# Three layer norms on VectorE, a pinned start of the stack, and the last pair's GLU one sequence at a time

## The chip, the core and the metric

The kernel runs on one core of a Trainium2 chip. A core has a matrix engine (TensorE, PE in the profile; its weight loads are shown apart as PEld), a vector engine (VectorE, DVE), an activation engine (ScalarE, ACT), a general engine (GpSimd, POOL) and SyncE (SP), which here issues nearly all DMA transfers. Each engine works through its own queue in program order and waits on semaphores for the others. The metric is the device time of one execution in microseconds; lower is better.

## The reference, cut to what matters

Sixteen sequences of 256 tokens with 128 features, float32, go through two blocks.

```python
x = x + causal_attention(layernorm(x))        # 16 heads of 8
x = x + stack(layernorm(x))                   # the stack's own input is the normalised x
# stack: six layers; every step sees shift_tokens(t): the upper 64 features come from the token before
for i in range(6):
    t = local_attention(shift_tokens(t)) + t  # 16 heads of 64, l2-normalised q and k, rotary, windows of 32 with the one before
    t = glu(shift_tokens(t)) + t              # layernorm over features, W1 (128 to 2*341), a*gelu(gate), W2 (341 to 128)
```

The layer norm divides by the root of the variance plus 1e-5. The GLU's gate uses the exact gelu.

## The kernel before, in words

**Two stages.** The first stage does the causal attention. Its loop `for s in range(-3, NSEQ + 3)` runs the steps of several sequences side by side and ends each round with `in_order(traced, True)`, which adds dependencies so that every compute engine takes the instructions of the round in the order in which the program emits them. `normed(s, "b")` (L162 to L179) is the layer norm between the two blocks: statistics and variance plus epsilon on VectorE (L168 to L171), the inverse root as a power on GpSimd (L84, called at L173), and the two halves of `xn_b`, 128x128 each, as a subtract and multiply on GpSimd (L176). `turned(s, "b")` transposes them on TensorE (L190) and ScalarE copies the result into `yT`, the stack's state with features on partitions (L194), one 128x512 tile for two sequences. `finish(s)` (L338 to L347) projects the attention's output, adds it to x and stores that sum to DRAM. `on(s - 3, normed, "b")` for sequence 15 is the last work of this stage.

**The stack.** Steps are numbered n = 16 * layer + sequence, from 0 to N - 1 = 95. `half(n, u)` (L795 to L854) emits half a step, u being 0 or 1, with pieces of several neighbours: `proj_qk` for step n + 2 (L472 to L499), `norms`, `roots`, `spread_k` and `norm_k` for n + 1, `sim`, `soften`, `power` and `proj_v` for n, `share`, `attn_T`, `attn_v` and `project_out` for what is older. Two sequences of one tile form a pair m, and its GLU runs in pieces spread over the following steps: `glu_shift` (L698), `glu_center` (L704), `glu_var` (L714), `glu_norm` (L725), three `glu_part` (L743) and `glu_out` (L760), each 512 columns wide. `leave(s)` (L767) transposes a finished sequence back, adds the sum stored in DRAM and stores the output.

**What sets the order.** For 0 <= n < 96, `in_order` pins each engine to the emitted order. For n = -2 and -1 (the first projections) and for n = 96 to 98 (the last GLU), it does not, and a scheduler places the instructions by its own estimate.

**The start of the stack.** `proj_qk(n, g, k)` multiplies the shifted sequence with one group of weights into PSUM (`qk`, L485), ScalarE squares it (L486), VectorE multiplies it with the rotary tables (`t12`, L487, 128x1024), and GpSimd adds the parts (`sq` at L496, `tq` twice at L499). `t12` has two buffers, so a new one waits until GpSimd has added the one before the last; `tq` has six, so the seventh waits until the first has left by DMA to `us` (L560). PSUM tiles of these steps come from a ring of four (`psum1`). `roots(0)` (L516 to L533) needs ScalarE's copy of the norms (L511), which stands behind the `yT` copies of sequences 14 and 15 on ScalarE; it computes the inverse root on VectorE with a seed and three Newton steps (L521 to L530), and GpSimd spreads it (`kb`, L533). `shift(n)` is two GpSimd copies and a memset (L464 to L466).

**The end of the stack.** ScalarE needs the table of Exp for `power` (L632) and that of Gelu for `glu_part` (L753); a switch is an instruction of its own in its queue. In the last steps, the output projection of sequence 15's second half (`wo`, L688, then the addition at L693) is followed by the GLU of pair 47, which holds sequences 14 and 15.

Of the kernel before, what the change touches and what calls it, by code (L numbers as in the profile page):

```python
# [38 lines left out]
def tile_transformer(  # L39
# [42 lines left out]
    def rsqrt(dst, src):  # L82
        n = dst.shape[-1]
        nc.gpsimd.tensor_tensor(dst, src, mhalf[:, :n], ALU.pow)  # L84

    last = {}
    engines = {e.engine for e in (nc.tensor, nc.vector, nc.scalar, nc.gpsimd)}
# [16 lines left out]
    with ExitStack() as st:  # L104
# [57 lines left out]
        def normed(s, tag):  # L162

            src = x1[s]
            stats = p4.tile([P, 2, 6], F32, tag="stats", name=f"st_{tag}{s}")
            mv = p4.tile([P, 2, 2], F32, tag="mv", name=f"mv_{tag}{s}")
            for t in range(2):
                nc.vector.bn_stats(stats[:, t, :], src[:, t, :])  # L168
                nc.vector.bn_aggr(mv[:, t, :], stats[:, t, :])
            var = p4.tile([P, 2], F32, tag="var", name=f"var_{tag}{s}")  # L170
            nc.vector.tensor_scalar(var, mv[:, :, 1], 1e-5, None, ALU.add)  # L171
            rstd = p4.tile([P, 2], F32, tag="rstd", name=f"rstd_{tag}{s}")
            rsqrt(rstd, var)  # L173
            xn = p2.tile([P, 2, E], F32, tag=f"xn{tag}", name=f"xn_{tag}{s}")
            for t in range(2):
                nc.gpsimd.tensor_scalar(  # L176
                    xn[:, t, :], src[:, t, :], mv[:, t, 0:1], rstd[:, t : t + 1], ALU.subtract, ALU.mult
                )
            xns1[s, tag] = xn  # L179
# [198 lines left out]
    with ExitStack() as st:  # L378
# [18 lines left out]
        def psum1(name):  # L397
            return ps_o.tile([P, 512], F32, tag="o", name=name)
# [115 lines left out]
        def roots(n, n2):  # L514
            ps = psum1(f"nT_{n}").rearrange("p (h g m) -> p h g m", h=4, g=4)
            for h in range(2):  # L516
                nc.tensor.transpose(
                    ps[:, h].rearrange("p g m -> p (g m)"), n2[:, h].rearrange("p a m -> p (a m)"), ident
                )
            x = p2.tile([P, 2, NG, 8], F32, tag="nx", name=f"nx_{n}")  # L520
            nc.vector.tensor_scalar(x, ps[:, 0:2, :, 0:8], 1e-24, None, ALU.max)  # L521

            y = p3.tile([P, 2, NG, 8], F32, tag="rn", name=f"rn_{n}")
            x_, y_ = (v.rearrange("p h g m -> p (h g m)") for v in (x, y))
            nc.vector.tensor_scalar(y_.bitcast(I32), x_.bitcast(I32), -0.5, 1597463007.0, ALU.mult, ALU.add)
            for _ in range(3):
                z = p4.tile([P, 64], F32, tag="nz", name=f"nz_{n}")
                nc.vector.tensor_tensor(z, x_, y_, ALU.mult)
                nc.vector.scalar_tensor_tensor(z, z, -0.5, y_, ALU.mult, ALU.mult)
                nc.vector.scalar_tensor_tensor(y_, z, 1.5, y_, ALU.add, ALU.mult)  # L530
            rn[n] = y
            kb = p1.tile([P, 2, NG, P], F32, tag="kb", name=f"kb_{n}")
            nc.gpsimd.tensor_copy(  # L533
                kb.rearrange("p h g (i d) -> p (h g) i d", d=32),
                y.rearrange("p h g m -> p (h g) m")[:, :, 4:8].unsqueeze(3).to_broadcast([P, 8, 4, 32]),
            )
            kbs[n] = kb
# [157 lines left out]
        x2s, bcs, sms = {}, {}, {}  # L695


        def glu_shift(m):  # L698
            b = m % 8
            x2 = x2s[m] = p1.tile([P, 2 * S], F32, tag="gl", name=f"x2_{m}")  # L700
            for i in range(2):
                shifted(x2[:, i * S : (i + 1) * S], 2 * b + i)

        def glu_center(m):  # L704
            x2 = x2s.pop(m)
            ps = psum1(f"cen_{m}")
            nc.tensor.matmul(ps, center, x2, start=True, stop=True)
            sq2 = p1.tile([P, 2 * S], F32, tag="h1", name=f"fsq_{m}")
            nc.scalar.activation(sq2, ps, AF.Square)
            xc = p1.tile([P, 2 * S], F32, tag="h2", name=f"xc_{m}")  # L710
            nc.scalar.copy(xc, ps)
            xns[m] = sq2, xc

        def glu_var(m):  # L714
            sq2, xc = xns[m]
            pv = psum1(f"pv_{m}")
            for t in range(4):
                nc.tensor.matmul(pv[:, t : t + 1], sq2[:, t * P : (t + 1) * P], mean1, start=True, stop=True)
            var = p4.tile([P, 4], F32, tag="var", name=f"var_{m}")
            nc.vector.tensor_scalar(var, pv[:, :4], 1e-5, None, ALU.add)  # L720
            rstd = p4.tile([P, 4], F32, tag="rstd", name=f"rstd_{m}")
            rsqrt(rstd, var)
            xns[m] = rstd, xc

        def glu_norm(m):  # L725
            l = m // 8
            rstd, xc = xns[m]
            ps = psum1(f"rs_{m}")
            for t in range(4):
# [8 lines left out]
            xn = p1.tile([P, 2 * S], F32, tag="xn", name=f"xn_{m}")  # L738
            nc.vector.tensor_tensor(xn, ps, xc, ALU.mult)
            nc.gpsimd.tensor_scalar(xn, xn, vecs[:, l, V_G : V_G + 1], vecs[:, l, V_B : V_B + 1], ALU.mult, ALU.add)  # L740
            xns[m] = xn

        def glu_part(mm, i):  # L743
            l = mm // 8
            if mm % 8 == 0 and i == 0:
                load_glu(l)
            xn = xns[mm]
            a, m = DI_PARTS[i]
            pg, ph = psum1(f"hg_{mm}_{i}"), psum1(f"ha_{mm}_{i}")
            nc.tensor.matmul(pg[:m], W["1"][:, DI + a : DI + a + m], xn, start=True, stop=True)  # L750
            nc.tensor.matmul(ph[:m], W["1"][:, a : a + m], xn, start=True, stop=True)  # L751
            g = p1.tile([P, 2 * S], F32, tag="gl", name=f"g_{mm}_{i}")
            nc.scalar.activation(g[:m], pg[:m], AF.Gelu, bias=vecs[:m, l, V_B1 + 3 + i : V_B1 + 4 + i])  # L753
            h = p1.tile([P, 2 * S], F32, tag=f"h{i}", name=f"h_{mm}_{i}")
            nc.vector.scalar_tensor_tensor(
                h[:m], ph[:m], vecs[:m, l, V_B1 + i : V_B1 + i + 1], g[:m], ALU.add, ALU.mult
            )
            hs[mm, i] = h

        def glu_out(mm):  # L760
            l, b = divmod(mm, 8)
            ps = psum1(f"w2_{mm}")
            for i, (a, m) in enumerate(DI_PARTS):
                nc.tensor.matmul(ps, W["2"][:m, i, :], hs[mm, i][:m], start=(i == 0), stop=(i == 2))  # L764
            nc.vector.scalar_tensor_tensor(yT[b], ps, vecs[:, l, V_B2 : V_B2 + 1], yT[b], ALU.add, ALU.add)

        def leave(s):  # L767

# [26 lines left out]
        def half(n, u):  # L795
            even = n % 2 == 0
            m = n // 2 - 1 if even else (n - 3) // 2
            glu = lambda m: 0 <= m < N // 2
            i, j = 2 * u, 2 * u + 1
            b, bu = (n, 0) if u else (n - 1, 1)  # L800
            bi, bj = 2 * bu, 2 * bu + 1
# [15 lines left out]
            do(n, soften, i)  # L817
            do(n, soften, j)
            do(n - 1, project_out, u)
            if u:  # L820
                do(n + 3, shift)
                if even and glu(m):
                    glu_shift(m)
            elif has(n + 1):
                roots(n + 1, n2s.pop(n + 1))
            do(b, attn_T, bi)
            do(b, attn_T, bj)
            do(n, proj_v, u, 0)
            do(b, attn_v, bi)
            if not even and u == 0 and glu(m):  # L830
                glu_center(m)
            do(n + 2, proj_qk, j, 0)
# [9 lines left out]
            if u == 0:  # L842
                do(n + 1, spread_k, 0)
                do(n + 1, norm_k, 0)
            do(n, power, i)
            do(n, power, j)
            do(b, attn_v, bj)
            do(*((n, masks, 1) if u == 0 else (n + 1, masks, 0)))
            if even and u and glu(m - 1):
                glu_out(m - 1)  # L850
                if m - 1 >= (DEPTH - 1) * 8:
                    leave(2 * ((m - 1) % 8))
                    leave(2 * ((m - 1) % 8) + 1)
            do(n, proj_v, u, 1)  # L854

        do(0, shift)
        last.clear()
        for n in range(-2, N + 3):
            for u in range(2):
                traced = len(nc.cur_bb.bb.instructions)  # L860
                half(n, u)
                in_order(traced, 0 <= n < N)

# [94 lines left out]
```

## Time and profile before

| | us |
|---|---|
| median of 3 runs | 3634.91 (3633.56 to 3640.62) |
| the profiled execution, as timed | 3631.49 |
| its span, first to last instruction | 3629.4 |
| first stage (causal attention), until its last `x` is added | about 376 |
| last GLU, from its centring to the last addition to `yT` | 3607.28 to 3625.15 |

The mean granted TensorE clock is 0.992. A line of the timeline gives the start in us, the duration in us, the engine with the source line, the operation, output and inputs, shapes and count; in brackets stands how long the engine was idle before and what ended the wait. A float32 matmul shows as two records (passes). `x8` merges eight records of one group.

Each step of the stack takes roughly a 96th of what lies between 440 and 3590 us, with TensorE busy 9 tenths or more in nearly every slice. The two ends are where engines wait for each other: around 368 to 420 us, and from 3587 us on.

### The profile page before, as it was taken

The page shows a single profiled execution, that of the slowest core. Times are in us where ns is not written, and L with a number is a line of the kernel's source. Part 1 is how long each engine was busy: PE and PEld are TensorE (multiplying, and loading weights), DVE is VectorE, ACT ScalarE, POOL GpSimd, SP SyncE. Part 2 cuts the span into 40 slices and gives each one's busy share as a digit, 9 for nine tenths or more (in the row PEclk, how much of TensorE's full clock was granted, in tenths as well). Part 3 has the DMA queues.
Part 4 walks back from the last instruction along what each step waited for, and adds up shares of the span by engine and source line. Part 5 has one row for each costly group of instructions (what it writes and reads, how often), then busy time and mean ns, then how long its engine had stood idle before and what let it go on. Part 6 is the DMA issues. An engine that isn't in the chain of part 4 may idle for free.

```text
span 3629.4 us, 153727 instructions
## 1 busy us (share of the span) xinstructions
PE 3485.9 (96%) x68032; PEld 2451.9 (68%) x68032; DVE 2841.1 (78%) x4866; ACT 1870.2 (52%) x3132; POOL 2592.8 (71%) x2731
## 2 busy tenths in 40 slices
PE   7999799999999999999999999999999999999998
PEld 5777466666666666666666666666676666666665
DVE  5765788887888888888877888877888888888784
ACT  2444355554555555555555555555555555555453
POOL 2221778778777778787777777778777877777772
PEclk9999899999999999999999999999999999999999
DMA  2000333334433334333334433334433343333342
GB/s 82 8 10 10 94 91 100 100 88 110 111 102 84 96 100 111 102 104 100 88 92 117 107 88 99 100 86 116 111 95 83 100 111 93 102 105 102 90 105 60
DMA packets 249444, 331.65 MB, mean 91 GB/s; under 512 B 74446, under 2 KB 105548, under 8 KB 247884
## 3 DMA queue, kind: packets, MB, share of 16 engines
q1 hardware_dynamic: 248060, 321.13, 33.1%
q8 instruction: 536, 8.78, 1.0%
q14 instruction: 128, 1.05, 0.1%
q10 hardware_dynamic: 720, 0.70, 0.1%
HBM read 28.12 MB, written 4.19 MB: 9 GB/s over the span
## 4 chain that ended last, share of the span: by engine, by line
PE 76%; DVE 9%; issue 7%; POOL 3%; ACT 2%; DMA 1%; SPq 0%; POOLq 0%; DVEq 0%; ACTq 0%
PE qk L485 17%; PE po L668 11%; PE v L568 9%; PE wo L688 8%; PE sim L605 6%; PE w L764 4%; PE hg L750 3%; PE ha L751 3%; PE aT L648 3%; PE n L506 2%; DVE tq L558 2%; DVE t L487 2%; PE bc L544 2%; PE sim L585 2%; ACT aT L650 1%
## 5 line engine op out<-in xcount | busy, mean ns | idle before, releaser
L487 DVE TENSOR_TENSOR t<-qk,ab 128x1024 f32<-128x1024 f32 x768 | 915.9, 1218 | 284.1 <-ACT sq L486 252.4
L499 POOL TENSOR_TENSOR tq<-t 128x512 f32<-128x512 f32 x768 | 962.1, 1274 | 85.4 <-DVE t L487 61.0
L485 PE MATMUL qk<-xs,wqk 128*128 128x256 f32 x3072 | 790.9, 393 | 1.6 <-DVE yT L693 1.5
L496 POOL TENSOR_TENSOR sq<-sq 128x512 f32<-128x512 f32 x384 | 489.1, 1274 | 282.3 <-ACT sq L486 272.3
L485 PEld LDWEIGHTS qk<-xs,wqk 128*128 128x128 f32 x3072 | 555.3, 191 | 146.9 <-issue 45.5
L486 ACT ACTIVATE sq<-qk 128x512 f32<-128x512 f32 x768 | 459.4, 599 | 377.3 <-PE qk L485 371.3
L650 ACT COPY aT<-aT 128x512 f32<-128x512 f32 x384 | 207.6, 587 | 599.4 <-PE aT L648 599.2
L668 PEld LDWEIGHTS po<-aT,vs 64*64 64x64 f32 x12288 | 327.8, 135 | 201.2 <-issue 106.8
L568 PE MATMUL v<-wv,xs 128*128 128x512 f32 x768 | 423.8, 634 | 28.1 <-ACT aT L650 21.2
L626 POOL TENSOR_TENSOR sm<-sm,mx 128x512 f32<-128x512 f32 x384 | 396.6, 1045 | 28.1 <-DVE mx L625 27.2
L605 PEld LDWEIGHTS sim<-us 64*32 64x32 f32 x24576 | 260.7, 105 | 205.9 <-issue 189.1
L668 PE MATMUL po<-aT,vs 64*64 64x32 f32 x12288 | 394.6, 222 | 5.2 <-issue 2.6
L668 PE MATMUL po<-aT,vn 64*64 64x32 f32 x12288 | 386.8, 219 | 4.6 <-issue 4.6
L574 ACT COPY vn<-v 128x512 f32<-128x512 f32 x384 | 225.3, 587 | 312.8 <-PE v L568 308.7
L688 PE MATMUL wo<-ao,wout 128*128 128x256 f32 x1536 | 383.2, 392 | 1.0 <-ACT ao L677 1.0
L642 POOL TENSOR_TENSOR ex<-ex,rec 128x512 f32<-128x512 f32 x288 | 317.5, 1116 | 39.7 <-ACT vn L574 18.2
L668 PEld LDWEIGHTS po<-aT,vn 64*64 64x64 f32 x12288 | 330.2, 136 | 5.1 <-issue 4.9
L605 PE MATMUL sim<-us 64*32 64x64 f32 (+1 forms) x24576 | 322.9, 221 | 3.1 <-DMA us<-tq 3.1
L688 PEld LDWEIGHTS wo<-ao,wout 128*128 128x128 f32 x1536 | 276.0, 189 | 49.5 <-ACT ao L677 1.7
L677 ACT COPY ao<-po 128x512 f32<-128x512 f32 x384 | 222.7, 580 | 114.9 <-PE po L668 114.9
L639 DVE TENSOR_REDUCE rec<-ex 128x8 f32<-128x512 f32 x384 | 252.0, 657 | 34.2 <-ACT ex L632 34.2
L625 DVE TENSOR_REDUCE mx<-sm 128x8 f32<-128x512 f32 x384 | 263.5, 686 | 13.3
(122 smaller groups left out, 5244.7 us busy)
## 6 DMA issues: line engine op xcount, KB each, us to landing
us<-tq SPq DMA_DIRECT2D x768, 256.0 KB
vs<-vn SPq DMA_DIRECT2D x384, 192.0 KB
vs<-vn SPq DMA_DIRECT2D x192, 64.0 KB
wqk<-in_f_wqkv_dram SPq DMA_DIRECT2D x96, 64.0 KB
ab<-in_tables_dram SPq DMA_DIRECT2D x6, 1024.0 KB
wv<-in_f_wqkv_dram SPq DMA_DIRECT2D x12, 256.0 KB
wout<-in_f_wo_dram SPq DMA_DIRECT2D x24, 128.0 KB
x<-in_x_dram SPq DMA_DIRECT2D x16, 128.0 KB
```

The lines of the kernel that those rows point to most:

```text
L485: nc.tensor.matmul(ps[:, t * S : t * S + S], W["qk", g][:, k, t, :], xs[n], start=True, stop=True)
L486: nc.scalar.activation(sq2[:, k].rearrange("p t n -> p (t n)"), ps, AF.Square)
L487: nc.vector.tensor_tensor(t12[:, k].rearrange("p f t n -> p f (t n)"), ps.unsqueeze(1).to_broadcast([P, 2, 2 * S]), W["ab", l][:, k].rearr ...
L496: nc.gpsimd.tensor_tensor(sq[n, g], sq2[:, :, 0, :], sq2[:, :, 1, :], ALU.add)
L499: nc.gpsimd.tensor_tensor(tq[n, g][:, t], t12[:, :, 0, t, :], t12[:, :, 1, 1 - t, :], ALU.add)
L568: nc.tensor.matmul(ps, xs[n][:, P * c : P * c + P], W["v"][:, u].rearrange("p g x d -> p (g x d)"), start=True, stop=True)
L605: nc.tensor.matmul(ps[WIN * r : WIN * r + WIN, x, col + first : col + 64], qk[part, g, 0, WIN * c : WIN * c + WIN], qk[part, g, 1, WIN * ( ...
L625: nc.vector.tensor_reduce(mx, seg, AX.X, ALU.max)
L626: nc.gpsimd.tensor_tensor(seg, seg, mx.unsqueeze(2).to_broadcast([P, 8, 64]), ALU.subtract)
L642: on.tensor_tensor(seg, seg, rec.unsqueeze(2).to_broadcast([P, 8, 64]), ALU.mult)
L668: nc.tensor.matmul(po[DH * y : DH * y + DH, h, x, g, WIN * r : WIN * r + WIN], v[64 * h : 64 * h + 64, r // 2, 2 * g + y, x, :], aT[64 * h ...
L688: nc.tensor.matmul(ps[:, :S].rearrange("p (h m) -> p h m", h=2), W["out"][:, g, 2 * u + x, :], a[:, x, :, g, :], start=(j == 0), stop=(j == 3)
```

## The change

Three edits, all at the ends.

**1. Layer norms of sequences 13, 14 and 15** (`normed(s, "b")` for s >= 13). The power on GpSimd becomes a seed and three Newton steps on VectorE, ten instructions on 128x2 (the same helper now also serves `roots`, with one buffer `nz` for its three steps where there were three), and the two 128x128 halves of `xn_b` go to VectorE too.

**2. The first steps of the stack in order.** `in_order(traced, -1 <= n < N)` pins n = -1 as well. The products of step 1, the norms of step 0 and the shift of sequence 2 then stand as emitted.

**3. The end.** `glu` no longer covers pair 47. Its GLU is called as a whole by `glu_all` for one sequence at a time (256 columns): sequence 14 at the end of `half(96, 0)`, sequence 15 in `half(96, 1)` after `project_out(95, 1)`. The last `glu_out` of pair 46 comes one half earlier. The last two `power` (step 95, the second pair of tiles) come before the first two `glu_part` of pair 46 and no longer after them.

```diff
+    def newton(y, x, z):
+        nc.vector.tensor_scalar(y.bitcast(I32), x.bitcast(I32), -0.5, 1597463007.0, ALU.mult, ALU.add)
+        for _ in range(3):
+            nc.vector.tensor_tensor(z, x, y, ALU.mult)
+            nc.vector.scalar_tensor_tensor(z, z, -0.5, y, ALU.mult, ALU.mult)
+            nc.vector.scalar_tensor_tensor(y, z, 1.5, y, ALU.add, ALU.mult)
...
-            rsqrt(rstd, var)
+            last_ones = tag == "b" and s >= NSEQ - 3
+            if last_ones:
+                newton(rstd, var, p4.tile([P, 2], F32, tag="rz", name=f"rz_{s}"))
+            else:
+                rsqrt(rstd, var)
             for t in range(2):
-                nc.gpsimd.tensor_scalar(
+                (nc.vector if last_ones else nc.gpsimd).tensor_scalar(
...
+        def which(m):
+            if isinstance(m, tuple):
+                return m[0] // 8, m[0] % 8, m[1] * S, S, f"{m[0]}_{m[1]}"
+            return m // 8, m % 8, 0, 2 * S, str(m)
...
+        def glu_all(m):
+            glu_shift(m)
+            glu_center(m)
+            glu_var(m)
+            glu_norm(m)
+            for i in range(3):
+                glu_part(m, i)
+            glu_out(m)
+            leave(2 * (m[0] % 8) + m[1])
...
-            glu = lambda m: 0 <= m < N // 2
+            glu = lambda m: 0 <= m < N // 2 - 1
...
             do(n - 1, project_out, u)
+            if n == N and u:
+                glu_all((N // 2 - 1, 1))
...
             do(b, attn_v, bi)
+            if n == N - 1 and u:
+                do(n, power, i)
+                do(n, power, j)
...
-            do(n, power, i)
-            do(n, power, j)
+            if n < N - 1 or u == 0:
+                do(n, power, i)
+                do(n, power, j)
...
-            if even and u and glu(m - 1):
+            if even and u == (n < N) and glu(m - 1):
                 glu_out(m - 1)
...
             do(n, proj_v, u, 1)
+            if n == N and u == 0:
+                glu_all((N // 2 - 1, 0))
...
-                in_order(traced, 0 <= n < N)
+                in_order(traced, -1 <= n < N)
```

The GLU's functions take the width from `which`, so a tuple (47, 0) or (47, 1) runs on 256 columns in tiles of the same size as before.

What the built programs hold, engine by engine, in words. VectorE, at the end of the first stage, has the ten steps for sequence 14 interleaved with the `t12` products of steps 0 and 1: seed, product, first step, product, second step and so on, five of the ten before the last of the products at that place, then the other five, then both halves of `xn_b`, and only then the addition of sequence 15. TensorE has the norms of step 0 before the transposes of sequence 14. GpSimd has the shift of sequence 2 (`xs_2`) between `tq` and `sq` of step 1's third and fourth groups; before, that shift stood in the middle of the first stage. At the end, TensorE's order is:

```
attn_v of step 95, last part
w2 of pair 46 (three matmuls), fin of sequences 12 and 13
cen, pv, rs, hg and ha three times, w2, fin      sequence 14, 256 columns
wo of step 95, second half (four matmuls)
cen, pv, rs, hg and ha three times, w2, fin      sequence 15, 256 columns
```

Everything between, steps 0 to 94, has the same instructions in the same order.

More of the change, by code (lines that the diff above doesn't have):

```diff
@@ L524, in roots @@
             x_, y_ = (v.rearrange("p h g m -> p (h g m)") for v in (x, y))
[L525 to L530, printed above, removed]
+            newton(y_, x_, p4.tile([P, 64], F32, tag="nz", name=f"nz_{n}"))
             rn[n] = y
@@ L695, in tile_transformer @@
         x2s, bcs, sms = {}, {}, {}
+        def which(m):
+            if isinstance(m, tuple):
+                return m[0] // 8, m[0] % 8, m[1] * S, S, f"{m[0]}_{m[1]}"
+            return m // 8, m % 8, 0, 2 * S, str(m)
         def glu_shift(m):
[L699 to L702, printed above, removed]
+            _, b, c0, w, name = which(m)
+            x2 = x2s[m] = p1.tile([P, 2 * S], F32, tag="gl", name=f"x2_{name}")[:, :w]
+            for i in range(w // S):
+                shifted(x2[:, i * S : (i + 1) * S], 2 * b + c0 // S + i)
         def glu_center(m):
             x2 = x2s.pop(m)
-            ps = psum1(f"cen_{m}")
+            _, _, _, w, name = which(m)
+            ps = psum1(f"cen_{name}")[:, :w]
             nc.tensor.matmul(ps, center, x2, start=True, stop=True)
-            sq2 = p1.tile([P, 2 * S], F32, tag="h1", name=f"fsq_{m}")
+            sq2 = p1.tile([P, 2 * S], F32, tag="h1", name=f"fsq_{name}")[:, :w]
             nc.scalar.activation(sq2, ps, AF.Square)
-            xc = p1.tile([P, 2 * S], F32, tag="h2", name=f"xc_{m}")
+            xc = p1.tile([P, 2 * S], F32, tag="h2", name=f"xc_{name}")[:, :w]
             nc.scalar.copy(xc, ps)
@@ L715, in glu_var @@
             sq2, xc = xns[m]
-            pv = psum1(f"pv_{m}")
-            for t in range(4):
+            _, _, _, w, name = which(m)
+            nt = w // P
+            pv = psum1(f"pv_{name}")
+            for t in range(nt):
                 nc.tensor.matmul(pv[:, t : t + 1], sq2[:, t * P : (t + 1) * P], mean1, start=True, stop=True)
-            var = p4.tile([P, 4], F32, tag="var", name=f"var_{m}")
-            nc.vector.tensor_scalar(var, pv[:, :4], 1e-5, None, ALU.add)
-            rstd = p4.tile([P, 4], F32, tag="rstd", name=f"rstd_{m}")
+            var = p4.tile([P, 4], F32, tag="var", name=f"var_{name}")[:, :nt]
+            nc.vector.tensor_scalar(var, pv[:, :nt], 1e-5, None, ALU.add)
+            rstd = p4.tile([P, 4], F32, tag="rstd", name=f"rstd_{name}")[:, :nt]
             rsqrt(rstd, var)
@@ L725, in glu_norm @@
         def glu_norm(m):
-            l = m // 8
+            l, _, _, w, name = which(m)
             rstd, xc = xns[m]
-            ps = psum1(f"rs_{m}")
-            for t in range(4):
+            ps = psum1(f"rs_{name}")[:, :w]
+            for t in range(w // P):
                 nc.tensor.matmul(
@@ L737, in glu_norm @@
                 )
-            xn = p1.tile([P, 2 * S], F32, tag="xn", name=f"xn_{m}")
+            xn = p1.tile([P, 2 * S], F32, tag="xn", name=f"xn_{name}")[:, :w]
             nc.vector.tensor_tensor(xn, ps, xc, ALU.mult)
@@ L743, in glu_part @@
         def glu_part(mm, i):
-            l = mm // 8
-            if mm % 8 == 0 and i == 0:
+            l, b, _, w, name = which(mm)
+            if b == 0 and i == 0:
                 load_glu(l)
@@ L748, in glu_part @@
             a, m = DI_PARTS[i]
-            pg, ph = psum1(f"hg_{mm}_{i}"), psum1(f"ha_{mm}_{i}")
+            pg, ph = psum1(f"hg_{name}_{i}")[:, :w], psum1(f"ha_{name}_{i}")[:, :w]
             nc.tensor.matmul(pg[:m], W["1"][:, DI + a : DI + a + m], xn, start=True, stop=True)
             nc.tensor.matmul(ph[:m], W["1"][:, a : a + m], xn, start=True, stop=True)
-            g = p1.tile([P, 2 * S], F32, tag="gl", name=f"g_{mm}_{i}")
+            g = p1.tile([P, 2 * S], F32, tag="gl", name=f"g_{name}_{i}")[:, :w]
             nc.scalar.activation(g[:m], pg[:m], AF.Gelu, bias=vecs[:m, l, V_B1 + 3 + i : V_B1 + 4 + i])
-            h = p1.tile([P, 2 * S], F32, tag=f"h{i}", name=f"h_{mm}_{i}")
+            h = p1.tile([P, 2 * S], F32, tag=f"h{i}", name=f"h_{name}_{i}")[:, :w]
             nc.vector.scalar_tensor_tensor(
@@ L760, in glu_out @@
         def glu_out(mm):
-            l, b = divmod(mm, 8)
-            ps = psum1(f"w2_{mm}")
+            l, b, c0, w, name = which(mm)
+            ps = psum1(f"w2_{name}")[:, :w]
             for i, (a, m) in enumerate(DI_PARTS):
                 nc.tensor.matmul(ps, W["2"][:m, i, :], hs[mm, i][:m], start=(i == 0), stop=(i == 2))
-            nc.vector.scalar_tensor_tensor(yT[b], ps, vecs[:, l, V_B2 : V_B2 + 1], yT[b], ALU.add, ALU.add)
+            y = yT[b][:, c0 : c0 + w]
+            nc.vector.scalar_tensor_tensor(y, ps, vecs[:, l, V_B2 : V_B2 + 1], y, ALU.add, ALU.add)
+        def glu_all(m):
[7 more added lines that the diff above has]
+            leave(2 * (m[0] % 8) + m[1])
         def leave(s):
```

## The prediction

> **What bounds the kernel now.** I read the page first, for where the time is not set by TensorE alone; then the chain that ended last for the two ends; then the timeline of each end, and the granted clock there. From the page, its first part and slices:
>
> ```profile
> span 3629.4 us, 153727 instructions
> ...
> PE 3485.9 (96%) x68032; PEld 2451.9 (68%) x68032; DVE 2841.1 (78%) x4866; ACT 1870.2 (52%) x3132; POOL 2592.8 (71%) x2731
> ...
> PE   7999799999999999999999999999999999999998
> ```
>
> TensorE is busy in nine tenths or more of every slice but three. The middle is TensorE's, and the change leaves its order alone, so I count only what happens around 350 to 420 us and after 3587 us; a delay at the first place moves everything behind it. The start, from the timeline:
>
> ```profile
> 381.15 3.70 POOL L499 TENSOR_TENSOR tq<-t 128x512 f32<-128x512 f32 x3
> 381.22 1.22 DVE L171 TENSOR_SCALAR var_b<-mv_b 128x2 f32<-128x2 f32 x1
> ...
> 387.61 0.47 PE L190 MATMUL lnT_b<-cst,xn_b 128*128 128x128 f32 x1 [7.37 <-POOL xn_b L176]
> ...
> 390.63 0.22 DVE L521 TENSOR_SCALAR nx<-nT 128x64 f32<-128x64 f32 x1 [8.18 <-PE nT L517]
> ...
> 402.37 4.96 POOL L499 TENSOR_TENSOR tq<-t 128x512 f32<-128x512 f32 x4 [0.91 <-DMA us<-tq]
> ...
> 403.62 3.42 PE L485 MATMUL qk<-xs,wqk 128*128 128x256 f32 x8
> ```
>
> TensorE waits 7.4 us for sequence 15's layer norm, whose GpSimd part stands behind `tq`. `nx` at 390.63 starts step 0's chain. At 402.37 GpSimd waits for a DMA that must free a `tq` buffer; at 403.62 step 2's products start. The second line matters: a 128x2 operation that takes 0.17 us elsewhere took 1.22 us and ended with the GpSimd instruction that ran beside it (381.15 plus 1.26). The end:
>
> ```profile
> 3587.32 1.28 ACT L753 ACT_TABLE_LOAD   x1
> ...
> 3590.89 1.28 ACT L632 ACT_TABLE_LOAD   x1
> ...
> 3597.80 1.28 ACT L753 ACT_TABLE_LOAD   x1
> ...
> 3607.28 1.02 PE L707 MATMUL cen<-x,cst 128*128 128x512 f32 x2
> ...
> 3614.16 2.08 PE L750 MATMUL hg<-xn,w 128*128 128x512 f32 x2 [1.76 <-POOL xn L740]
> ...
> 3624.40 0.75 DVE L765 SCALAR_TENSOR_TENSOR yT<-w,vecs,yT 128x512 f32<-128x512 f32 x1 [1.83 <-PE w L764]
> ```
>
> Three table loads, then one GLU of 17.87 us from `cen` to the end of `yT` (3625.15). It is latency: 6.88 us before `hg`, with TensorE nearly idle. The granted clock there, by stretches of 1 us:
>
> ```profile
> 3613.00:3614.00 1.00, 0.00 (x0) 0.00 (x0) 0.23 (x1) 0.00 (x0) 0.66 (x1) 0.50 0.00 0
> ...
> 3617.00:3618.00 1.00, 1.00 (x3) 0.48 (x2) 0.00 (x0) 0.02 (x1) 0.00 (x0) 0.50 0.00 0
> ...
> 3619.00:3620.00 1.00, 1.00 (x4) 0.47 (x3) 0.00 (x0) 0.69 (x1) 0.00 (x0) 1.00 0.00 0
> ```
>
> The third number from the right is the clock: half speed for the first 4.4 us of `hg` and `ha` (3614.16 to 3618.55), a pass of 512 columns then taking 0.85 us instead of 0.43.
>
> **The start, part by part.** *Sequence 13.* Its variance ends at 350.93 with GpSimd idle. Before: power 0.72 and two halves 1.58, transposes at 352.70 and 353.47. After: ten VectorE steps. The row nearest is 0.17 us for 128x2 and 0.26 from start to start for 128x64; I take 0.20, 2.0 us (bounds 1.7 and 2.6). A half of `xn_b` on VectorE is not in the trace; between 0.17 (128x2) and 0.80 (GpSimd's), nearest is 0.29 (128x128, L323); two take some 0.5. Ready at 353.4: nothing gained or lost.
>
> *Sequence 14.* Here VectorE's order decides. The first five Newton steps stand between `t12` products, and these wait for GpSimd's `tq` (two buffers). Without the power, GpSimd goes `sq` 363.50, `tq`, `sq` twice (to 369.74), `tq` (372.25), `sq` (373.5), `tq` (376.0), 1.26 us each. So the products run at 372.5, 375.0, 376.5 and 379.2, the last ends at 380.4. Every Newton step reads two SBUF tiles, and while GpSimd works such a step gets in only between two of its instructions: besides 381.22, a seed at 3509.45 took 0.49 and the next step 1.00 us beside GpSimd's pair at 3508.86 (2.05), the seven after that 0.22 each. Two or three of the last five steps therefore wait for `tq` of step 1 (380.4 to 382.9): chain done at 383.8, both halves at 384.4. If no step waited, it would be 380.1; if each waited a whole instruction, 386. I take 384.4: both rows of the trace wait. Before it was 374.42.
>
> The Trainium skill ("GPSIMD Engine Reference", section 8, Key points) says that GpSimd shares its SBUF interfaces with VectorE and contends with instructions that have two SBUF inputs or use both ports; the row at 381.22 agrees, and the rule speaks against this change: by it the chain ends at 384.4, without it at 380.1.
>
> *Sequence 15.* From the second half of 14 to the addition of x it was 1.42 us (374.42 to 375.84): 385.8. Addition and statistics 1.6, steps 2.0, halves 0.5, GpSimd idle now: 389.9; it was 388.33. From the transposes to `nx` 2.25 us before, with a mask matmul of 0.58 between, 1.9 without: `nx` at about 392.0, **1.4 us late**. The norm itself shrinks from 12.5 to 4.1 us after its addition; that addition comes 10 us later.
>
> *Shift of sequence 2.* `kb`, the spread and the first `us` transfers follow `nx` in the old order, so the DMA that frees `tq` ends at about 403.7 (402.28 plus 1.4). Then GpSimd does `tq` (2.51) and now the shift (0.98, as at 430.48) before anything else: step 2's `xs` at 407.2, its products at 407.3 instead of 403.62, **3.6 us late**. Before, the shift was long done. Everything that followed 403.62 (squares, `t12` of step 2, `soften`, `roots(1)`) follows again; TensorE then waited 5.2 us for `kb` of step 1, so no slack takes it up. The transfer took 5.1 us among the weight loads; two 128 KB loads of `res` no longer stand between them, and I put 0.4 us back: **3.2 us** for the start. Bounds: no VectorE step waits, 0.2 us gained; all wait, 5.5 us lost.
>
> **The end, part by part.** *Exp earlier.* The two exponentials (1.15) go before the Gelu table; the loads at 3590.89 and 3597.80 go. By hand: Gelu's first `g` ends at 3590.5, `h` 3591.25, second `g` 3592.03, copies after it 1.2 us early; `hg` of part 2 at 3595.2, last `attn_v` at 3598.0 instead of 3600.30: **2.3 us gained** of 2.56.
>
> The skill ("ScalarE: Activation LUTs", What ACT_TABLE_LOAD costs) gives 1.28 us for a load plus 1.38 for a drain; the trace has the load and 0.02 us after it, so the measurement decides for 1.28; an estimate from the page's figure would make the two loads 5.3 us.
>
> *Order.* `wo` (8 passes, 2.0 us) leaves its place ahead of `w2` of pair 46: `w2` from 3599.07, `yT` 3601.75, `cen` 1.30 after that: 3603.05, 4.2 us early. *One half GLU:* `cen` 0.63, square 0.37 (128x256, L194) plus 0.05, `pv` 0.55, to the power 0.31, power 0.72 (128x2) plus 0.05, `rs` 0.6, `xn` 0.42 (L693) plus 0.1, GpSimd 0.6 (between 0.39 and 0.77) plus 0.05: 4.4. Then 12 passes of 256 columns: 4.4 us at half clock hold ten at 0.43, the rest 0.4: 4.8. `w2` 1.3, 0.28 and addition 0.42: 2.0. Together 11.2, where the whole pair took 17.87: halves cost more than half. *Two of them in a row:* sequence 14 ends at 3614.25; TensorE's order has `fin` (0.35) and `wo` (1.75) only now, then the addition (0.47) and shift (0.95) that the second half waits for: `cen` at 3617.8, end at 3629.0 against 3625.15, **3.85 us late**. One store less at the very end gives back 0.4: **3.4 us** lost. Bounds from the clock: full speed in both halves, 0.6 us gained; half speed throughout, 7.0 lost.
>
> **Sum.** 3629.4 + 3.2 + 3.4 = 3636.0 for the span, 3638.1 as that execution was timed (3631.49). That execution lies 3.4 us under the median of the runs, 3634.91, and the runs are what is compared, so I name 3634.9 + 6.6 = **3641.5 us**. A measurement of this kernel can tell about 0.2% (7.3 us) from no change, so this counts as no change, just.
>
> **Rivals.** *Slower beyond that:* the clock. If it stays at half through `hg`, `ha` and `w2` of both halves, each costs 1.8 us more: 3645.1. It decides from 0.7 us on. For: TensorE is thinly used for 4.4 us of each chain, and before the clock was already falling between 3611 and 3612 us (0.83), 3.5 us after `cen`. Against: it returned 4.4 us after `hg` began. *Less slow:* VectorE's steps don't wait for GpSimd; the start then gives 0.2 us: 3638.1. For: the median Newton step of the trace takes 0.225 us. Against: the rows at 381.22, 3509.45 and behind it. *Faster, as the change reads:* `wo` is not held and the halves overlap, so that one chain of 11.2 and some 2 us of the other follow `wo`: the end 6.7 us early, and with the start 2.6 early, 3625.6. For: sequence 14's part of `yT` is ready at 3585.1 (L693 at 3584.69). Against: TensorE's built order is serial, and `nx` cannot precede 388.0.
>
> **Chances.** Forecast 0.50 (3638 to 3645; 0.30 of it within 0.2%, 0.20 slower), clock 0.18 (slower), no waits 0.18 (same), overlap 0.10 (faster), else 0.04 (0.01 faster, 0.02 same, 0.01 slower). So 0.11 faster, 0.50 same, 0.39 slower. The range leaves out the overlap and the far end of the clock case: 3632 (both lower bounds, 0.2 and 0.6 gained, and 2 us for the spread of the runs) to 3648 (5.5 and 7.0 lost).
>
> **What would show it.** Right: `xn_b` of sequence 14 at about 384, some of its steps near 1 us; `nx` at 392; `qk` of step 2 behind the shift at 407; one table load after 3587; `cen` of sequence 15 more than 14 us after that of 14. Wrong: `nx` before 390, or `wo` beside sequence 14's GLU.

## The result and the profile after

| | before | changed |
|---|---|---|
| median of 11 runs each, us | 3634.34 (3631.36 to 3640.62) | 3641.07 (3636.54 to 3649.15) |
| ratio, 95% interval | | 1.0021 (1.0012 to 1.0030) |
| the profiled execution, as timed, and its span | 3631.49, 3629.4 | 3636.54, 3634.6 |
| first `hg` of pair 46 to the end of the last `yT` | 38.57 | 44.57 |

The changed kernel is about 7 us slower, at the edge of what a measurement can tell; forecast were 3641.5. But the sum came out right with its two halves wrong in opposite directions: the start costs less than forecast, the end more. That the total lies within 1 us of the forecast is partly luck. First the page of the changed kernel, the lines that answer to the first fence of the prediction:

```profile
span 3634.6 us, 153818 instructions
...
PE 3484.8 (96%) x68052; PEld 2455.6 (68%) x68052; DVE 2852.1 (78%) x4908; ACT 1868.2 (51%) x3135; POOL 2582.7 (71%) x2724
...
PE   7999699999999999999999999999999999999998
```

TensorE's busy time is the same (3485.9 before); the lost time is idle time, and no slice of 91 us shows it. So to the two ends. VectorE's timeline around the norm of sequence 14 in the changed kernel:

```profile
368.53 1.30 DVE L88 TENSOR_SCALAR rstd_b<-var_b 128x2 int32<-128x2 int32 x1
369.75 1.21 DVE L500 TENSOR_TENSOR t<-qk,ab 128x1024 f32<-128x1024 f32 x1
370.88 0.17 DVE L90 TENSOR_TENSOR rz<-var_b,rstd_b 128x2 f32<-128x2 f32 x1
372.29 1.22 DVE L500 TENSOR_TENSOR t<-qk,ab 128x1024 f32<-128x1024 f32 x1 [1.24 <-POOL tq L512]
...
378.50 1.17 DVE L92 SCALAR_TENSOR_TENSOR rstd_b<-rz,rstd_b 128x2 f32<-128x2 f32 x1
379.71 1.19 DVE L90 TENSOR_TENSOR rz<-var_b,rstd_b 128x2 f32<-128x2 f32 x1
380.93 1.18 DVE L91 SCALAR_TENSOR_TENSOR rz<-rz,rstd_b 128x2 f32<-128x2 f32 x1
...
382.34 0.60 DVE L189 TENSOR_SCALAR xn_b<-x,mv_b,rstd_b 128x128 f32<-128x128 f32 x2
384.36 0.42 DVE L357 TENSOR_TENSOR x<-pr,x 128x256 f32<-128x256 f32 x1 [1.42 <-PE pr L356]
```

GpSimd beside it:

```profile
378.40 1.26 POOL L509 TENSOR_TENSOR sq<-sq 128x512 f32<-128x512 f32 x1
379.62 2.48 POOL L512 TENSOR_TENSOR tq<-t 128x512 f32<-128x512 f32 x2
```

Five of the ten steps on 128x2 (the fifth, not shown, at 373.44) take 1.17 to 1.30 us beside GpSimd's adds, and end with them (378.50 plus 1.17 is 379.67, the add's end 379.66; 380.93 plus 1.18 is 382.11, against 382.10); alone, one takes 0.16. x of sequence 15 follows at 384.36 (375.84 before). What comes of it, in the same timeline:

```profile
390.54 0.22 DVE L534 TENSOR_SCALAR nx<-nT 128x64 f32<-128x64 f32 x1 [2.02 <-PE nT L530]
...
400.89 2.49 POOL L512 TENSOR_TENSOR tq<-t 128x512 f32<-128x512 f32 x2 [1.27 <-DMA us<-tq]
403.33 0.39 POOL L477 COPY xs<-yT 64x256 f32<-64x256 f32 x1
...
404.34 3.78 PE L498 MATMUL qk<-xs,wqk 128*128 128x256 f32 x8
```

`nx` is not late (390.63 before). The DMA that frees `tq` ends 1.5 us earlier than before (400.89 against 402.37), so the shift behind it costs step 2's products only 0.7 us (403.62 before). The end, in the chain of waits and in the timeline:

```profile
3592.79 4.31 DMA vs<-vn
...
3597.23 0.90 PE po L675 x48
```

```profile
3588.11 1.28 ACT L769 ACT_TABLE_LOAD   x1
...
3604.33 0.60 PE L721 MATMUL cen<-x,cst 128*128 128x256 f32 x2
...
3615.56 1.89 PE L695 MATMUL wo<-ao,wout 128*128 128x256 f32 x8
...
3618.86 0.70 PE L721 MATMUL cen<-x,cst 128*128 128x256 f32 x2 [1.41 <-POOL x L479]
...
3623.53 1.22 PE L766 MATMUL hg<-xn,w 128*128 128x256 f32 x2 [1.27 <-POOL xn L756]
...
3630.41 0.48 DVE L782 SCALAR_TENSOR_TENSOR yT<-w,vecs,yT 128x256 f32<-128x256 f32 x1 [0.86 <-PE w L780]
```

One table load is left of three. But the last parts of `attn_v` now wait for `vs`, a transfer of 4.31 us that the table loads used to cover. Then two GLUs in a row, `wo` between them: 3604.33 to 3615.23 and 3618.86 to 3630.89. The granted clock (third number from the right) in the second one:

```profile
3621.00:3622.00 1.00, 0.26 (x2) 0.19 (x2) 0.00 (x0) 0.00 (x0) 0.68 (x1) 0.97 0.00 0
3622.00:3623.00 1.00, 0.26 (x2) 0.00 (x0) 0.42 (x1) 0.00 (x0) 0.07 (x1) 0.50 0.00 0
...
3628.00:3629.00 1.00, 1.00 (x4) 0.76 (x3) 0.00 (x0) 0.47 (x1) 0.00 (x0) 0.61 0.00 0
```

It is at half from the end of 3621 to 3628.8, over all of `hg` and `ha`.

**The middle is not as still as its instructions.** They are the same in both kernels, yet, on the clock of each execution, the changed one is 2.05 us late at the last `aT` of the start (426.42 against 424.37), 0.5 at the first `cen` (504.24, 503.75), 3.8 at pair 45's (3515.01, 3511.18) and 0.26 us early at the first `hg` of pair 46 (3586.32, 3586.58). Part of it shows as stretches at half clock, which lie elsewhere in each execution; here is one in the kernel before, which the changed one's execution doesn't have at that place:

```profile
3557.00:3560.00 3.00, 2.60 (x73) 2.10 (x74) 0.00 (x0) 1.98 (x4) 0.03 (x1) 0.51 0.57 139
3560.00:3563.00 3.00, 3.00 (x4) 1.33 (x5) 0.00 (x0) 0.00 (x0) 0.00 (x0) 0.50 0.00 1
```

So the two spans cannot be subtracted to 1 us. Below, each end is measured from an instruction close to it: the end from the first `hg` of pair 46 to the end of the last `yT`, the start from the addition of x of sequence 14.

### The profile page after: what moved, and what is told of

Its sections match the earlier page's. It is cut to its first block, busy times and chain, and to the rows that moved or that the text cites. A ratio compares the mean times of both kernels' runs of the same rounds, so it can differ in the third digit from the quotient of the medians.

```text
span 3634.6 us, 153818 instructions
## 1 busy us (share of the span) xinstructions
PE 3484.8 (96%) x68052; PEld 2455.6 (68%) x68052; DVE 2852.1 (78%) x4908; ACT 1868.2 (51%) x3135; POOL 2582.7 (71%) x2724
## 4 chain that ended last, share of the span: by engine, by line
PE 81%; DVE 9%; issue 4%; ACT 2%; POOL 2%; DMA 1%; SPq 0%; POOLq 0%; DVEq 0%; ACTq 0%
PE qk L498 17%; PE po L675 11%; PE v L575 9%; PE wo L695 8%; PE sim L612 6%; PE w L780 4%; PE hg L766 3%; PE ha L767 3%; PE aT L655 3%; PE n L519 2%; DVE tq L565 2%; PE bc L551 2%; DVE t L500 2%; PE sim L592 2%; ACT aT L657 1%
## 5 line engine op out<-in xcount | busy, mean ns | idle before, releaser
L632 DVE TENSOR_REDUCE mx<-sm 128x8 f32<-128x512 f32 x384 | 263.4, 686 | 13.3
```

The source lines that it names most:

```text
L632: nc.vector.tensor_reduce(mx, seg, AX.X, ALU.max)
```

## The experiments

**Theory A** (mine): the end costs, since two half-width GLUs stand one behind the other with the projection held between them, and the start costs little. **Rivals:** B, the start costs; C, the half clock is what costs; D, the transfer of `vs` takes back what the earlier exponentials gain.

**e1, the third edit alone.**

```diff
-            last_ones = tag == "b" and s >= NSEQ - 3
+            last_ones = False
...
-                in_order(traced, -1 <= n < N)
+                in_order(traced, 0 <= n < N)
```

> Start as before, third edit alone. Theory A (the end costs: two half-width GLUs in a row, the second held by the output projection): from the first hg of pair 46 to the end of the last yT 44.6 us as in the changed kernel (38.6 before); the time about 5.5 us over before, 3640. Theory B (the start costs, the end is neutral): 38.6 us there and the time within 1 us of before, 3634. Theory C (the half clock costs): 44.6 only where the clock is at 0.50 through hg and ha of both halves; some 41 us where it is at 1.00.

Measured: 3639.93 against 3637.31 of before, ratio 1.0011 (1.0001 to 1.0021); 45.04 us at the end, the first half with `hg` and `ha` wholly at half clock (12 passes in 5.3 us). As A; the interval of the time, 0.4 to 7.6 us, holds A's 5.5.

**e2, the first and second edit alone.** The end of the kernel before: pair 47 whole, the last two `power` behind `glu_part`.

```diff
-            glu = lambda m: 0 <= m < N // 2 - 1
+            glu = lambda m: 0 <= m < N // 2
...
-            if n == N - 1 and u:
-                do(n, power, i)
-                do(n, power, j)
...
-            if even and u == (n < N) and glu(m - 1):
+            if even and u and glu(m - 1):
```

> First and second edit alone, the end as before. Theory A: the last aT of the start (424.4 us before, 426.4 in the changed kernel) at about 426.4, 38.6 us from the first hg of pair 46 to the last yT, and the time 0 to 2 us over before, 3634 to 3636.5, which the runs can hardly tell from nothing. Theory B (the start costs all of it): 5 to 7 us over before, 3640.

Measured: 3636.93 against 3637.31, ratio 1.0000 (0.9989 to 1.0011); 38.56 us at the end. B falls: the interval ends at 4 us, and it asks for 5 to 7. The last `aT` of the start is as late as in the changed kernel, as A says; it stands in the table under e11.

**e3, the earlier exponentials alone.** e1 with pair 47 whole (the `glu` lines of e2), the two `power` kept early.

> Only the two exponentials of step 95 go ahead of the Gelu table; norms, start and the last pair's GLU as before. By the prediction's step (two table loads of 1.28 us gone, nothing late in their place) the last attn_v starts 11.4 us after the first hg of pair 46 (13.7 before) and the time falls by 2.3 us. By theory D (the transfer of vs for the last attn_v is now late and eats half) it starts at 12.8 us and the time falls by 1 us, 3633.3; taken alone the runs can't tell either from nothing, the trace can.

Measured: the last `attn_v` starts 12.14 us after the first `hg` (13.72 before, 12.77 in the changed kernel), and 37.05 us at the end: 1.5 us gained, between the two figures. TensorE waits 0.64 us for `vs` here and 1.27 us in the changed kernel's row (`po` at 3597.23). The time, 3633.78 against 3637.31 (0.9989, 0.9980 to 0.9999), is under before. D holds in part: of 2.3 us the transfer takes back a third here (0.7) and about half with the changed end (1.35 in the changed kernel, 1.1 in e1 and e11, which wait 1.01 and 1.07 us).

**e4, the two halves overlapped in buffers of their own.** Each half's tiles are eight slots of one `t12` tile; the order of n = 96 is written out:

```diff
+            return own[m][:, slots.index(what) % 8, :]
...
+            if n == N and u:
+                glu_part(e, 0)
             do(n - 1, project_out, u)
-            if n == N and u:
-                glu_all((N // 2 - 1, 1))
+            if n == N:
+                glu_shift(f if u else e)
+            if n == N and u:
+                glu_part(e, 1)
+                glu_part(e, 2)
+                glu_center(f)
+                glu_out(N // 2 - 2, 0, 1)
+                glu_var(f)
+                glu_out(N // 2 - 2, 1, 3)
+                glu_norm(f)
+                glu_out(e)
...
-                in_order(traced, -1 <= n < N)
+                in_order(traced, 0 <= n <= N)
```

Here e is sequence 14's half and f sequence 15's; `cen`, `pv` and `rs` of e stand between the parts of `attn_T` and `attn_v` of step 95.

> Start as before, exponentials early, and the two half-width GLUs of the last pair overlapped: each half in a buffer of its own (one t12 tile), sequence 14's begun right after the first half of the output projection, the second half of the projection before most of it, and w2 of pair 46 and of sequence 14 put between the steps of sequence 15's chain; engines pinned to the emitted order up to n = 96. Theory A (serial order and shared single buffers cost, halves themselves don't): hg of pair 46 to the last yT about 29.5 us (38.6 before, 44.6 in the changed kernel), time about 9 us under before, 3625. Theory C (thin use of TensorE keeps the clock at half, whatever the order): 33 us or more. If half-width chains cost by themselves: 36 us or more.

Measured: 3628.65 against 3637.31, ratio 0.9974 (0.9964 to 0.9984), and 31.43 us at the end. Its timeline there:

```profile
3601.05 0.70 PE L735 MATMUL cen<-own,cst 128*128 128x256 f32 x2 [0.25 <-POOL own L479]
...
3608.01 1.89 PE L695 MATMUL wo<-ao,wout 128*128 128x256 f32 x8
...
3611.46 0.68 PE L735 MATMUL cen<-own,cst 128*128 128x256 f32 x2
...
3617.00 0.70 PE L780 MATMUL hg<-own,w 128*128 128x256 f32 x2
```

Sequence 14's `cen` comes 10.1 us after the first `hg` of pair 46 (18.0 in the changed kernel), while TensorE still works on step 95. `wo` now stands in the first chain, not behind it, and `cen` of 15 comes 10.4 us after that of 14 instead of 14.5. TensorE's clock is at full speed in every 1 us stretch from 3598 to 3624. Forecast were 29.5 us, so the overlap is worth less than I put. The halves by themselves were not the mistake; what cost was that they run one behind the other. The order and the buffers were changed together here, so this run doesn't tell which of the two weighs more, and part of its gain is the clock.

**e5 and e6, the first and the second edit alone,** each with the end of before (the lines of e2, and the one line of e1 for the other edit).

> First edit alone: the three norms on VectorE, n = -1 not pinned, the end as before. Measured from the addition of x of sequence 13 (343.96 us before, 343.87 in the changed kernel): step 2's first products 59.7 us later before, 60.5 in the changed kernel; the last aT of the start 80.4 and 82.5. Theory A1 (the shift of sequence 2 behind the adds on GpSimd makes the start late, the norms don't): 59.7 and 80.4 here, although x of sequence 15 is added 8 us later than before. Theory B1 (the norms make it late): 60.5 and 82.5 here.

> Second edit alone: n = -1 pinned, the norms on GpSimd, the end as before. Theory A1: step 2's first products 60.5 us after the addition of x of sequence 13 and the last aT 82.5 us after it. Theory B1: 59.7 and 80.4.

**e11, the changed kernel once more,** unaltered.

> The changed kernel itself once more, beside before and the two kernels above on one chip. Theory A: 6 to 7 us over before (6 us of the end, 0.6 us of the start), ratio about 1.0018. By the medians of e1 (1.0011) and e2 (1.0000) added up: 4 us, 1.0011.

e5 to e8 are single executions and are read by their traces, not by their times. The reference point I chose moved: from the addition of sequence 13 to that of 14 it is 12.0 us in the kernel before and 13.3 in e1, whose instructions are the same up to there. The clock goes with it: 12.0 to 12.2 us where the granted clock between the two additions is 1.00 (before, e3, e4, changed, e2), 13.3 to 14.0 us in the nine others, where it is 0.81 to 0.89. From the addition of 14 (us; the clock is the granted one over 340 to 430 and 430 to 510):

| kernel | `nx` of step 0 | step 2's products | last `aT` of the start | first `cen` | clock |
|---|---|---|---|---|---|
| before, e3, e4 (old start) | 34.7 | 47.5 to 47.9 | 68.4 | 147.7 to 147.8 | 0.87, 0.98 |
| e1, e10 (old start) | 33.2 to 33.3 | 46.5 | 68.1 to 68.2 | 146.0 to 146.1 | 0.81, 1.00 |
| norms alone (e5) | 34.46 | 47.23 | 68.15 | 148.93 | 0.81, 0.96 |
| pin alone (e6) | 32.78 | 46.77 | 67.74 | 145.58 | 0.80, 1.00 |
| changed, e2 (both edits) | 34.5 | 48.3 | 70.4 | 148.2 to 148.3 | 0.83, 1.00 |
| e11, e7, e8 (both edits) | 34.3 to 34.6 | 48.3 to 48.7 | 69.2 to 69.5 | 147.1 to 147.4 | 0.77, 1.00 |

Neither A1 nor B1. From the addition of 13, as the expectations count, e5 gives 60.9 and 81.8 us and e6 60.2 and 81.2, which is neither theory's pair for either run; from that of 14, each edit alone costs nothing at the last `aT`, and the two together are 0.8 to 2.3 us later than the old start, in all five executions that have both. How I read it, without a run that shows it by itself: the norms make `nx` about 1 us late (e5 against e1), the pin puts the shift of 1 us behind `tq`, and the start has room for one. In e6 the shift does set when step 2 begins, which shows in the wait, and still it isn't late:

```profile
406.15 2.72 PE L498 MATMUL qk<-xs,wqk 128*128 128x256 f32 x8 [2.15 <-POOL xs L479]
```

Against the kernel before itself the changed one is 2.0 us late there, but only 0.4 us at the first `cen` (148.2 against 147.8): between them TensorE's clock is 0.98 in the one and 1.00 in the other. Over all five executions of the old start and all five of both edits the first `cen` is 0.5 us later in the mean if counted from the addition of 14 and 1.3 us if counted from that of 13 (160.4 to 161.4 against 159.3 to 159.8). So the start costs about 0.5 to 1.3 us. e11 as a whole: 3644.72 against 3636.22, ratio 1.0019 (1.0009 to 1.0029), with 45.06 us at the end.

**e7, the held projection ahead of both halves.**

```diff
                 do(n - 1, project_out, u)
             if n == N and u:
+                glu_all((N // 2 - 1, 0))
                 glu_all((N // 2 - 1, 1))
...
-            if n == N and u == 0:
-                glu_all((N // 2 - 1, 0))
```

> The changed kernel with the second half of the output projection ahead of both half-width GLUs instead of between them; everything else the same, buffers shared as before. From the first hg of pair 46 to the end of the last yT (44.6 us in the changed kernel): if holding the projection between the halves costs its 3.6 us, the second cen follows w2 of sequence 14 at once and it is about 41.7; if that time is only moved ahead of the first half, 44.6; in both the second half still waits for the first one's buffers, so nothing near e4's 31.4.

Measured: 41.98 us at the end, 2.6 less than in the changed kernel. Of this 0.8 us lie within the two chains (22.1 us together, 22.9 there), whose stretches at half clock fall differently; holding `wo` itself costs some 1.8 us. The second `cen` begins 0.27 us after the first half's `fin` does, and still the halves are serial.

**e8, idle products in TensorE's waits.**

```diff
+        def fill(w):
+            nc.tensor.matmul(psum2("fill")[:, 0, :w], center, W["1"][:, :w], start=True, stop=True)
...
+            if m[1]:
+                fill(512)
             glu_center(m)
+            fill(256)
             glu_var(m)
+            fill(512)
             glu_norm(m)
+            fill(512)
...
-                in_order(traced, -1 <= n < N)
+                in_order(traced, -1 <= n <= N)
```

> The changed kernel with idle products (seven matmuls of 256 or 512 columns into a PSUM tile that nothing reads) in TensorE's waits before hg of each half; n = 96 pinned so that they stand there. Theory C (thin use of TensorE halves the clock in the chains): 1.00 through hg, ha and w2 of both halves, and hg of pair 46 to the last yT about 40 us instead of 44.6. Theory A (latency of the serial halves, the clock a small part): the clock may rise, but the time stays above 42.5.

Measured: 41.48 us, between the two figures, and the clock at full speed throughout both chains (stretches of 2 us; the first number is TensorE's busy time):

```profile
3624.00:3626.00 2.00, 1.87 (x7) 0.65 (x6) 0.44 (x2) 0.00 (x0) 0.70 (x1) 1.00 0.00 0
...
3628.00:3630.00 2.00, 2.00 (x11) 1.59 (x11) 0.97 (x2) 0.77 (x3) 0.00 (x0) 1.00 0.00 0
```

A chain from `cen` to the end of `yT` takes 9.8 and 9.9 us (10.9 and 12.0 in the changed kernel). The pin of n = 96 moves nothing ahead of them: the first `cen` comes 17.99 us after the first `hg`, 18.01 in the changed kernel. So the half clock is 3.1 us of this end; without it the halves still take 2.9 us more than the whole pair did, at that pair's own half clock.

**e9, e10 and e12: what beats both kernels.** e9 is e4 with n = -1 pinned. e10 keeps pair 47 whole and the exponentials early, and puts idle products (256, 512, twice 512 columns) in the waits, with n = 96 to 98 pinned. e12 is e9 with two norms on VectorE:

```diff
-            last_ones = tag == "b" and s >= NSEQ - 3
+            last_ones = tag == "b" and s in (13, 15)
```

> e4 with n = -1 pinned as well (the second edit, which alone brought the last aT of the start 0.5 us earlier against a run of the same clock pattern, e6 against e1); norms on GpSimd as before. Theory A: hg of pair 46 to the last yT 31.4 us as in e4, the time 8 to 9.5 us under before, 3628 where before is 3637; the 0.5 us can't be told from e4 by the times. If e4's gain was the luck of its chip: within 0.2% of before.

> Start as before, exponentials early, pair 47's GLU whole in 512 columns as before, with four idle products (one of 256, three of 512 columns) in TensorE's waits before its hg; n = 96 to 98 pinned so that they stand there. From e3 (hg of pair 46 to the last yT 37.1 us, hg to ha at half clock for about 5 us) and e8 (the fills gained 3.1 us in two halves): if the clock comes back with the fills, about 34.5 us there and the time 4 us under before; if the clock doesn't pay here, 37. Against e4: 34.5 would leave 3 us to the overlap of the two halves alone.

> e9 with the norms of sequences 13 and 15 on VectorE and that of sequence 14 on GpSimd, where its steps would stand between the adds. From the addition of x of sequence 14 (355.95 us before, 356.03 in the changed kernel): x of 15 added 19.4 to 20 us later as before (28.3 in the changed kernel), nx of step 0 at about 31 (34.7 before, 34.5 changed), the last aT of the start at about 66.5 (68.4 before, 70.4 changed). Theory A2 (VectorE's steps of sequence 14, each waiting for a GpSimd instruction, make the start late): so it goes, and the time is 1 to 2 us under e9's 0.998 of before, which the times can't tell. Rival (any norm on VectorE beside the pinned adds is late): nx at 34 or later and the last aT at 69 or later.

| | time | before beside it | ratio, 95% interval | end | last `aT` of the start |
|---|---|---|---|---|---|
| e9 | 3627.68 | 3636.22 | 0.9980 (0.9971 to 0.9989) | 31.47 | 67.57 |
| e10 | 3631.59 | 3636.22 | 0.9988 (0.9979 to 0.9997) | 35.49 | 68.13 |
| e12 | 3628.13 | 3636.30 | 0.9978 (0.9969 to 0.9987) | 31.51 | 67.45 |

e9 and e12 repeat e4's gain on other runs: 8 us under before, and e9 17 us under the changed kernel that ran beside it (e11). In e10 the chain from `cen` to `yT` falls from 17.93 us (e3) to 15.43, but the pinned order puts all of `wo` ahead of `w2` of pair 46 and takes 0.9 back; what the overlap is worth beyond the clock is then 3 to 4 us. It also answers C: the whole pair loses 2.5 us to the half clock itself, the two halves 3.1, and with idle products in both the halves in a row end 6.0 us later (41.48 against 35.49). So the half clock is not what makes the halves lose. In e12 x of 15 comes 19.84 us after 14's, as forecast, and the start keeps e9's place; but `nx` is at 33.0 and not at 31, since sequence 15's own first steps fall beside GpSimd's adds:

```profile
383.69 1.14 DVE L88 TENSOR_SCALAR rstd_b<-var_b 128x2 int32<-128x2 int32 x1
384.86 1.18 DVE L90 TENSOR_TENSOR rz<-var_b,rstd_b 128x2 f32<-128x2 f32 x1
...
387.29 0.16 DVE L92 SCALAR_TENSOR_TENSOR rstd_b<-rz,rstd_b 128x2 f32<-128x2 f32 x1
```

The rival of e12 (34, and 69 for `aT`) falls, and my size of the gain was too large. e9 and e12 can't be told apart by their times.

## Why the prediction was right, and where it was not

- **Sequence 13: right.** Both halves of `xn_b` done at 353.5 (forecast 353.4; 353.42 before).
- **Sequence 14: right in kind, put 1.5 us too late.** Three of the last five steps wait, as said, and both halves are done at 382.94, not 384.4. (The row at 381.22 that the term leans on reads one SBUF tile; that steps which read two wait shows at 378.50, 379.71 and 380.93.) The products of `t12` between them ran earlier than I put them: the last ended at 378.4, not 380.4.
- **`nx` 1.4 us late: wrong in this execution, about right in others.** It came at 390.54, 0.1 us early against the kernel before. From the addition of 13 it stands at 46.6 to 46.7 us in all five executions of the old start, at 46.7 in the changed kernel and e2, and at 48.3 to 48.6 in e11, e7 and e8, whose clock was lower.
- **Shift of sequence 2, 3.6 us late: the step that failed at the start.** It was 0.7 us. I let the transfer that frees `tq` follow `nx` at the old distance (403.7, less 0.4 for the loads of `res` that left); GpSimd went on at 400.89. Some 1.5 us of this is `nx`; the rest is the transfer, here in the chains of before and of the changed kernel:

```profile
397.12 5.10 DMA us<-tq
397.07 3.66 DMA us<-tq
```

  It takes 5.1 to 5.4 us in the six executions without the pin, where a load of `res` is issued between the two groups of `us`, and 3.65 in the changed kernel, e2, e9 and e12, where the pin leaves it behind both. So this change of order, which I put at 0.4 us, goes with 1.4, and the second edit pays back part of its own shift. The place was right, the wait for the shift shows in e6 as well. The term of 3.2 us measures about 0.5 to 1.3.
- **Exp earlier, 2.3 us gained: the step that failed at the end.** By hand I moved everything behind the table loads and left out the one transfer on that path, `vs`; 0.95 us is left in the changed kernel, 1.1 to 1.2 in e1, e7 and e11, 1.6 in e3.
- **Half GLU 11.2 us: right for the first (10.9), short for the second (12.0),** whose `hg` and `ha` ran wholly at half clock (12.0 and 11.6 in e1 and e11). I had the clock as a rival, at 1.8 us more for a half wholly at half clock; it is 1.1 (12.0 against 10.9). Full speed in both halves takes 3.1 us away (e8), where my bound took away 4.0.
- **3.5 us between the halves, 0.4 us for the shorter store: right** (3.63 and 0.54).
- **The end, 3.4 us lost:** 6.0 us to the last `yT`, less 0.5: 5.5 us, and 6.5 us in e1 and e11 to the last `yT`.

So 3.2 + 3.4 became about 1 + 5.5, and the two errors cancelled. The bounds held both: the start's ran from 0.2 gained to 5.5 lost, the end's from 0.6 gained to 7.0 lost.

What is left open: how much of the 0.8 to 2.3 us at the start is the edits' and how much the place of the stretches at half clock, which differs between the groups of the table. The old start's two places of `nx` there (34.7 and 33.3) are the reference point's: from the addition of 13 they are one. Nor did I try to shorten the transfer of `vs`, or to give the halves buffers of their own without a new order.

## What to carry to other kernels

Cutting the last, lonely piece of work in two pays only if the second piece runs beside the first: look at TensorE's built order and at every buffer that both pieces use before counting on it (44.6 us in a row, 31.4 us overlapped, 37.1 us uncut with the same early exponentials). When an instruction is removed from a path, list all that was late beneath it, transfers first. And two edits that cost nothing alone can cost something together.

## What the hardware showed that I had not expected

- **Idle products pay.** Seven matmuls that nothing reads made the end 3.1 us shorter, since the clock stays up. TensorE's waits before the clock fell were short: in the changed kernel none between 3617.5 and 3623.5 is reported longer than 1.41 us, at busy shares of 0.14 to 0.61 per us. The Trainium skill ("TensorE: Matmul & The Clock Gate", HAM oscillation) puts the rule as avoiding idle gaps over about 3.4 us; here thin use was enough, and the measurement decides. The same page (Part 1) has the clock judged in free-running windows of 3413 ns, and the stretch at half clock here, 6.8 us by the rows, is two of them.
- **A small VectorE instruction beside GpSimd takes GpSimd's time.** 128x2 steps: 0.16 us alone, 1.14 to 1.30 beside 128x512 adds of 1.26, with whose end they end; also the seed, which has one input from SBUF; the products of 128x1024 with one input from PSUM took 1.21 to 1.22 us at the same time, no more than elsewhere (1.16 to 1.22).
- **An unchanged middle moves by some us.** From 0.5 us late at the first `cen` to 3.8 late and then 0.3 early, between two executions of the same 3000 us of instructions.
